# A transformer block on one core: the linear quotient written as a mean less a small term

## The chip, the cores and the metric

One core of one Trainium2 chip runs one program. The metric is device time in microseconds, the median of repeated executions; less is better. Each kernel also has one execution taken with the hardware profiler.

## The reference, cut to what matters

The input `x` is 8 batches of 512 tokens by 128 features. Four residual parts follow one another: a linear attention with 16 heads of 64 (1024 columns), an FP4 feed-forward of width 352, a causal softmax attention with 16 heads of 8, and 8 experts of which each token takes two. The part that changes is the first:

```python
q = einsum(x, wq) + bq;  k = einsum(x, wk) + bk;  v = einsum(x, wv) + bv
Q = elu(q) + 1.0;        K = elu(k) + 1.0
KV   = sum over tokens of K * v        # one number per head column
Ksum = sum over tokens of K            # one number per head column
Z    = 1.0 / (Q * Ksum + 1e-6)
attn = Q * KV * Z
out  = gelu(attn @ wo + bo)            # added to x
```

`KV` and `Ksum` are elementwise along a head's columns, so each of the 1024 columns has its own two scalars per batch.

## The kernel before, in words

The block goes through the 8 batches. Everything of the first part stands transposed: columns on the 128 partitions, the 512 tokens along the free dimension. The 1024 columns make 8 tiles of 128 by 512.

The code doesn't issue instructions where they are written. Each call makes a `Step` in a `Plan`: it records its engine, what it needs, which buffers it takes, and an estimated cost from `cost()`. The stages of a batch belong to lanes (`loads`, `norm`, `linear`, `out`, `fp4`, `attention`, `routing`, `experts`). A stage is run inside a `Span`, which gives its steps ranks that rise evenly from a low to a high number; the pairs are in the table `TURNS`, one for each lane and batch. `Plan.ordered()` then simulates the engines with the estimated costs: of the steps that could start, an engine takes the one with the lowest rank (with a bonus for the step that empties a PSUM buffer), if its buffers are free. A step on `nc.either` may go to VectorE or GpSimd. The result is one fixed order per engine, which the chip then carries out with semaphores. `SBUF` (line 661 on) lists how many buffers each tag has.

`kept_warm()` goes through that order and, where the plan shows TensorE idle, inserts at most one zero product (a matmul of `zeros` by `ident` into the PSUM tile `mid`, which adds nothing). Its length is the gap or what is missing to a share `TARGET` of a recent window, whichever is less.

In `linear_attention` (line 978), `elu` makes one tile of a feature: a matmul, a ScalarE Relu and Exp with the bias, and a VectorE combination, which gives elu without the added one. `features(c)` does this for K (the accumulated sum gives `ks`), multiplies K by v (giving `kv`), and does it for Q. ScalarE then adds one to Q, makes the divisor z = Q · Ksum + 1e-6, and scales the tile of `wo` by `kb`, the KV of that column with the bias of v in it. `products(c)` takes two tiles together, so that one reciprocal serves both:

```python
r = z0 * z1;  q0 = q0 * z1;  q1 = q1 * z0
r = 1 / r                       # two halves of 256
q0 = q0 * r;  q1 = q1 * r       # Q0/z0 and Q1/z1
```

`linear_out` (line 1031) multiplies the eight tiles by the eight scaled tiles of `wo` in two accumulations of four, adds the bias, applies gelu, transposes and adds to `x`. The FP4 stage, the softmax attention (`group`, in which a group is 4 heads), the routing and the experts follow, each in its own lane, so that the work of several batches is under way at once.

Of the kernel before, what the change touches and what calls it, by code (L numbers as in the profile page):

```python
# [134 lines left out]
class Plan:  # L135
# [51 lines left out]
    def span(self, lane, low, high):  # L187
        return Span(self, lane, low, high)
# [60 lines left out]
    def ordered(self):  # L249
# [15 lines left out]
        empties = set()  # L265
        for s in self.steps:
            for b in s.uses:
                if b.tag in self.psum and s.engine != "tensor" and (False or max(b.users, key=lambda u: u.number) is s):
                    empties.add(s)
# [14 lines left out]
        while done < len(self.steps):  # L284
            for e in self.HOP:
                while busy[e] <= now:
# [4 lines left out]
                    for s in sorted(  # L291
                        ready,
                        key=lambda s: (s.rank - (ahead if s.work > 0.6 * s.cost else 0.0) - (EMPTY if s in empties else 0.0), s.number),
                    ):
                        if s.port and port > now:
                            continue
                        asked = {}
                        for b in s.takes:
                            asked.setdefault(b.tag, []).append(b)
                        if not all(  # L300
                            all(b in turns[s.lane, t][-len(bs) :] for b in bs)
                            for t, bs in asked.items()
                        ):
                            continue
                        if all(
                            (t not in kept or stuck) and free.has(t, len(bs)) for t, bs in asked.items()
                        ):
                            best = s
                            break

                        kept.update(asked)
# [53 lines left out]
    def kept_warm(self, order):  # L365
# [11 lines left out]
        for s in order:  # L377
            if s.engine == "tensor" and self.warmer is not None:
# [6 lines left out]
                if want > 0.2 and not any(a - 0.5 < last < b + 0.1 for a, b in read):  # L385
                    n = min(512, 64 * int(want / 1.7e-3 / 64))
                    f = Step(-1, "tensor", None)
                    f.calls, f.cost, f.work = self.warmer(n), n * 1.7e-3, n * 1.67e-3
                    f.start, f.end = last, last + f.cost
                    past.append((f.start, f.end, 1.0))  # L390
                    out.append(f)
                last = s.end
# [116 lines left out]
class Span:  # L509


    def __init__(self, plan, lane, low, high):
        self.plan, self.lane, self.low, self.high = plan, lane, low, high
# [5 lines left out]
    def __exit__(self, *_):  # L519
        steps = self.plan.steps[self.first :]  # L520
        total, done = sum(s.cost for s in steps) or 1.0, 0.0
        for s in steps:
            s.rank = self.low + (self.high - self.low) * done / total
            done += s.cost
# [88 lines left out]
def cost(engine, method, out, ins, a, k):  # L613
# [32 lines left out]
    if engine == "gpsimd":  # L646
# [20 lines left out]
    ("xnT", [P, S], 2, F32),  # L667
    ("kf", [P, S], 2, F32),
    ("qf", [P, S], 7, F32),
    ("z", [P, S], 3, F32),  # L670
    ("r", [P, S], 1, F32),
    ("y", [P, S], 2, F32),
    ("wk_o", [P, D], 5, F32),
# [12 lines left out]
    ("oT", [P, NT, P], 2, F32),  # L686
# [18 lines left out]

TURNS = {
    "loads": (
        (-3.318, -1.909), (-0.316, -0.059), (0.897, 0.897), (1.614, 1.925),
        (2.836, 3.009), (4.433, 4.682), (4.978, 4.978),
    ),  # L710
    "norm": (
        (-2.124, -2.124), (-0.875, -0.875), (0.083, 0.200), (1.422, 1.904),
        (2.231, 2.231), (3.002, 3.606), (3.880, 4.108), (5.162, 5.409),
    ),
    "linear": (
        (-1.500, -0.940), (-0.500, 0.050), (0.419, 0.790), (2.088, 2.088),
        (2.612, 3.162), (3.422, 3.979), (4.158, 4.730), (4.805, 5.222),
    ),
    "out": (
        (-1.176, -0.826), (-0.386, -0.123), (0.618, 0.709), (1.508, 1.508),  # L720
        (2.508, 3.214), (3.335, 3.734), (4.601, 4.985), (5.739, 6.093),
    ),
    "fp4": (
        (-1.986, -1.736), (-0.900, -0.500), (0.154, 0.510), (1.010, 1.218),
        (2.103, 2.516), (3.487, 3.887), (3.993, 4.270), (5.177, 5.177),
        (5.602, 6.278),
    ),
    "attention": (
        (-0.500, 0.000), (0.000, 0.909), (0.934, 1.761), (2.198, 3.044),
        (3.241, 3.877), (3.954, 4.849), (5.114, 5.848), (6.017, 7.017),  # L730
        (7.193, 8.226),
    ),
    "routing": (
        (1.913, 2.213), (2.979, 3.308), (4.000, 4.223), (5.196, 5.230),
        (6.538, 6.538), (7.103, 7.746), (8.148, 8.148), (8.956, 9.346),
    ),
    "experts": (
        (2.400, 2.713), (3.217, 3.986), (4.222, 5.211), (5.438, 6.138),
        (6.531, 6.863), (7.391, 8.138), (8.571, 9.439), (9.499, 10.378),
# [5 lines left out]
def block_kernel(  # L745
# [141 lines left out]
    rank = const.tile([P, NT, E], F32, name="rank", tag="rank")  # L887
    for e in range(E):
        dev.gpsimd.memset(rank[:, :, e : e + 1], float(E - e))
# [3 lines left out]
    dev.gpsimd.memset(one_sb, 1.0)  # L893

# [83 lines left out]
    def linear_attention(b):  # L978

        xnT = normed.pop(b)  # L980

        def elu(c, i, w, tag, **accum):
# [10 lines left out]
        def features(c):  # L993

            ks, kv, kb = (new("s1", [P, 1]) for _ in range(3))
            kf = elu(c, 1, wqkv[1], "kf", accum_out=ks)
            nc.vector.tensor_scalar(ks, ks, float(S), None, ALU.add)
# [4 lines left out]
            nc.vector.scalar_tensor_tensor(pw, kf, 1.0, pw, ALU.add, ALU.mult, accum_out=kv)  # L1002

            nc.vector.tensor_scalar(
                kb, ks, bqkv_sb[:, 2, c : c + 1], kv, ALU.mult, ALU.add
            )
            qf = elu(c, 0, wqkv[0], "qf")
            nc.scalar.activation(qf, qf, AF.Identity, bias=one_sb)
            z = new("z", [P, S])
            nc.scalar.activation(z, qf, AF.Identity, bias=eps_sb, scale=ks)  # L1010
            wk_o = new("wk_o", [P, D])
            nc.scalar.activation(wk_o, wo_sb[c // 2][:, c % 2, :], AF.Copy, scale=kb)
            return qf, z, wk_o

        def products(c):


            (q0, z0, w0), (q1, z1, w1) = features(c), features(c + 1)
            r = new("r", [P, S])
            nc.either.tensor_tensor(r, z0, z1, ALU.mult)  # L1020
            nc.either.tensor_tensor(q0, q0, z1, ALU.mult)
            nc.either.tensor_tensor(q1, q1, z0, ALU.mult)
            for part in (slice(0, 256), slice(256, S)):
                nc.vector.reciprocal(r[:, part], r[:, part])
            nc.either.tensor_tensor(q0, q0, r, ALU.mult)
            nc.either.tensor_tensor(q1, q1, r, ALU.mult)
            return [(w0, q0), (w1, q1)]

        return [p for c in range(0, NC0, 2) for p in products(c)]

    def linear_out(b, pairs):
        y = new("y", [P, S])
        for half in range(2):
            po = new("ahead", [P, S])
            with together():
                for i, (wk_o, qz) in enumerate(pairs[4 * half : 4 * half + 4]):
                    nc.tensor.matmul(po, wk_o, qz, start=(i == 0), stop=(i == 3))
            if half == 0:
                nc.scalar.activation(y, po, AF.Identity, bias=bo_sb)
            else:  # L1040
                nc.vector.tensor_tensor(y, po, y, ALU.add)
# [454 lines left out]
    for b in range(NB):  # L1496
# [3 lines left out]
        pairs = stage("linear", linear_attention, b)  # L1500
        stage("out", linear_out, b, pairs)
# [80 lines left out]
```

## Time and profile before

| | |
|---|---|
| median of 3 runs | 1132.38 us (1130.52 to 1133.14) |
| the profiled execution | 1131.95 us, span 1130.1 us |
| busy: TensorE matmul, VectorE, ScalarE, GpSimd | 92%, 73%, 56%, 55% |
| mean granted TensorE clock | 0.982 |
| reciprocals on `r` | 64, 110.3 us of VectorE |
| zero products | 88 records, 40.4 us of TensorE |
| DMA | 44.31 MB, mean 39 GB/s |
| first and last reciprocal on `r` | 26.5 and 775.3 us |
| first maximum of scores in the softmax attention | 173.6 us |

Every planned instruction stands at line 407, where the plan issues it, so the profile's groups are told apart by the names of their tiles: `r`, `qf` and `z` are the linear attention, `pair` and `pr` the scores, `act` and `um` the experts. `ahead` is a PSUM bank that many stages use. An fp32 matmul of the program appears as two records. In a row of groups the numbers after the bar are busy microseconds, mean nanoseconds of one instruction, and the engine's idle time just before them with its releaser. A row of a stretch has the stretch, its length, each engine's busy time with the number of instructions, the granted TensorE clock in parts of one, the share of the DMA engines, and GB/s. A row of waits has who waited, for whom, total microseconds, how many times, and the longest.

### The profile page before, as it was taken

To read this page: it belongs to the slowest core of one execution; us is meant where nothing else is said; L and a number is where in the kernel's file an instruction comes from. 1 tells how busy PE (TensorE), PEld (TensorE's weight loads), DVE (VectorE), ACT (ScalarE), POOL (GpSimd) and SP (SyncE) were. 2 spreads that over 40 slices of the span, in tenths; PEclk is the share of its full clock that TensorE was granted. 3 is DMA by queue.
4 is the path that set the end of the run, shared out by engine and by line. 5 is a ranking of instruction groups with operands and counts; after the bars stand their busy time and mean duration, and the time that the engine had idled before them with its cause. 6 is when DMAs were issued, how large, how long until landed. Compare 5 with 4: busy or idle time off the path is not lost.

```text
span 1130.1 us, 15043 instructions
## 1 busy us (share of the span) xinstructions
PE 1040.2 (92%) x5025; PEld 488.0 (43%) x5025; DVE 830.3 (73%) x1868; ACT 630.8 (56%) x1084; POOL 624.3 (55%) x669
## 2 busy tenths in 40 slices
PE   6667788998899999999998999999999999999998
PEld 2223333344344444444543444454454445445454
DVE  6868879897888967758788968788667765556543
ACT  5756787678786644644578555764443443344311
POOL 6647846676676466237635755467644533441534
PEclk9879989999999999999999999999999999999999
DMA  8000030001101020111012000210002102001000
GB/s 235 1 1 0 1 111 1 21 20 56 39 20 30 10 94 20 58 72 35 26 39 94 19 21 20 95 30 19 20 7 98 39 20 104 21 20 30 1 10 9
DMA packets 30572, 44.31 MB, mean 39 GB/s; under 512 B 4192, under 2 KB 18464, under 8 KB 30496
## 3 DMA queue, kind: packets, MB, share of 16 engines
q1 hardware_dynamic: 30496, 43.37, 11.9%
q8 instruction: 39, 0.64, 0.2%
q14 instruction: 37, 0.30, 0.1%
HBM read 23.95 MB, written 18.87 MB: 38 GB/s over the span
## 4 chain that ended last, share of the span: by engine, by line
PE 57%; DVE 15%; ACT 6%; issue 2%; POOL 1%; DMA 0%; POOLq 0%; DVEq 0%; ACTq 0%
PE ahead L407 31%; PE pair L407 19%; PE mid L407 7%; ACT pr L407 2%; DVE r L407 2%; DVE mx L407 2%; DVE h L407 1%; DVE sc L407 1%; ACT qf L407 1%; DVE s4 routing L407 1%; DVE qf L407 1%; DVE act L407 1%; ACT z L407 1%; DVE kf L407 1%; DVE oh L407 1%
## 5 line engine op out<-in xcount | busy, mean ns | idle before, releaser
L407 ACT ACTIVATE pr<-pair 128x1024 f32<-128x1024 f32 (+1 forms) x192 | 166.7, 879 | 149.2 <-PE pair L407 129.1
L407 DVE TENSOR_REDUCE mx<-pair 128x4 f32<-128x512 f32 (+2 forms) x192 | 198.5, 1041 | 68.4 <-PE pair L407 57.7
L407 POOL TENSOR_SCALAR_AFFINE_SELECT pr<-pr 128x256 f32<-128x256 f32 (+1 forms) x192 | 92.8, 485 | 176.4 <-ACT pr L407 175.6
L407 PE MATMUL pair<-qkT 32*128 32x128 f32 (+7 forms) x1024 | 172.3, 387 | 9.4 <-ACT pr L407 2.7
L407 PEld LDWEIGHTS pair<-qkT 32*128 32x128 f32 (+1 forms) x1024 | 84.4, 183 | 181.8 <-ACT pr L407 52.0
L407 POOL TENSOR_TENSOR act<-act,tw 128x512 f32<-128x512 f32 x64 | 81.3, 1272 | 88.8 <-DVE act L407 80.6
L407 PE MATMUL ahead<-um,b_sb 128*128 128x512 f32 x240 | 122.2, 607 | 0.0
L407 DVE RECIPROCAL r<-r 128x256 f32<-128x256 f32 x64 | 110.3, 1736 | 14.9 <-POOL r L407 14.8
L407 DVE SCALAR_TENSOR_TENSOR act<-act,ahead 128x512 f32<-128x512 f32 x120 | 81.9, 684 | 51.4 <-ACT act L407 38.0
L407 POOL TENSOR_TENSOR qa<-qa,qa 128x704 f32<-128x704 f32 (+4 forms) x60 | 81.2, 1354 | 35.1 <-DVE qa L407 26.2
L407 POOL TENSOR_TENSOR qf<-qf,r 128x512 f32<-128x512 f32 x64 | 80.5, 1278 | 34.5 <-DVE r L407 27.8
L407 PE MATMUL mid<-pr,va 128*10 128x512 f32 (+3 forms) x1024 | 93.3, 435 | 0.0
L407 POOL TENSOR_TENSOR qf<-qf,z 128x512 f32<-128x512 f32 x64 | 80.3, 1270 | 0.0
L407 ACT ACTIVATE act<-ahead 128x512 f32<-128x512 f32 x60 | 35.8, 597 | 72.0 <-PE ahead L407 71.9
L407 PE MATMUL ahead<-act,a_sb 128*128 128x512 f32 x128 | 65.2, 619 | 0.0
L407 POOL TENSOR_TENSOR r<-z,z 128x512 f32<-128x512 f32 x32 | 40.9, 1278 | 41.6 <-ACT z L407 39.3
L407 PE MATMUL ahead<-tT,w_sb 128*128 128x512 f32 x120 | 63.3, 609 | 0.0
L407 ACT ACTIVATE ahead<-ahead,bqkv_sb 128x512 f32<-128x512 f32 x96 | 63.0, 656 | 0.0
L407 PE MATMUL pair<-mask_q,ident 128*128 128x128 bf16 (+1 forms) x384 | 61.6, 242 | 0.0
L407 PE MATMUL ahead<-xnT,wk 128*128 128x512 f32 x100 | 56.7, 650 | 4.8 <-DVE kf L407 2.1
L407 PEld LDWEIGHTS ahead<-um,b_sb 128*128 128x128 f32 x240 | 40.7, 190 | 36.1 <-issue 29.6
L407 ACT ACTIVATE z<-qf,eps_sb,s 128x512 f32<-128x512 f32 x64 | 51.9, 811 | 6.8 <-DVE s L407 5.1
(227 smaller groups left out, 1986.4 us busy)
## 6 DMA issues: line engine op xcount, KB each, us to landing
stacks<-qk SPq DMA_DIRECT2D x32, 512.0 KB
qkT<-stacks SPq DMA_DIRECT2D x128, 128.0 KB
x<-in SPq DMA_DIRECT2D x8, 256.0 KB
qkT<-mr SPq DMA_DIRECT2D x128, 4.0 KB
out<-x SPq DMA_DIRECT2D x8, 256.0 KB
w_sb<-in SPq DMA_DIRECT2D x3, 256.0 KB
wq<-in SPq DMA_DIRECT2D x4, 128.0 KB
wk<-in SPq DMA_DIRECT2D x4, 128.0 KB
```

The source lines that it names most:

```text
L407: getattr(e, method)(*a, **k)
```

## The change

The quotient Q · KV / (Q · Ksum + 1e-6) is written as KV/Ksum · (1 − 1e-6 / (Q · Ksum + 1e-6)). The first factor, `mean`, is one number per column, so its product with `wo` is one column of 128 numbers per batch, made by eight matmuls of one column; 1e-6 times the second part comes from the eight large matmuls, which now take 1/z in place of Q/z. Q itself is no longer multiplied. Four tiles share one reciprocal: u = z0 z1, v = z2 z3, r = 1/(u v), then u r = 1/v and v r = 1/u, and each 1/z is its partner times one of them.

`ks`, `kv` and `mean` become columns of one [128, 8] tile per batch, and the small steps are done for two columns at once; part of them move to GpSimd. The bias of v is added to `mean`. In `linear_out` the two sums are scaled by −1e-6, and the mean column with the output bias is added by one more ScalarE pass.

Beside it: `Span` takes three ranks (low, middle, high), and `TURNS` has new numbers throughout; buffer counts change; `kept_warm` fills pauses longer than 1.5 us in the plan to four fifths, with several zero products of up to 512 columns; the bonus of a step that empties a PSUM buffer is worked out from the buffers that steps take; some constants are set in another order at the start.

```diff
 def kept_warm(self, order):
...
                 want = min(gap, TARGET * Clock.WINDOW - worked)
-                if want > 0.2 and not any(a - 0.5 < last < b + 0.1 for a, b in read):
+
+                if gap > 1.5:
+                    want = max(want, 0.8 * gap)
+                while want > 0.2 and not any(a - 0.5 < last < b + 0.1 for a, b in read):
                     n = min(512, 64 * int(want / 1.7e-3 / 64))
...
                     out.append(f)
+                    last, want = f.end, want - f.cost
...
 class Span:
...
-            s.rank = self.low + (self.high - self.low) * done / total
+            x = done / total
+            s.rank = (
+                self.low + (self.middle - self.low) * 2 * x if x < 0.5
+                else self.middle + (self.high - self.middle) * (2 * x - 1)
+            )
...
-    ("xnT", [P, S], 2, F32),
+    ("xnT", [P, S], 1, F32),
     ("kf", [P, S], 2, F32),
-    ("qf", [P, S], 7, F32),
-    ("z", [P, S], 3, F32),
-    ("r", [P, S], 1, F32),
+    ("qf", [P, S], 9, F32),
+    ("heads", [P, NC0], 9, F32),
+    ("r", [P, S], 3, F32),
     ("y", [P, S], 2, F32),
-    ("wk_o", [P, D], 5, F32),
+    ("wk_o", [P, D], 8, F32),
...
-    ("oT", [P, NT, P], 2, F32),
+    ("oT", [P, NT, P], 1, F32),
...
     "linear": (
-        (-1.500, -0.940), (-0.500, 0.050), (0.419, 0.790), (2.088, 2.088),
-        (2.612, 3.162), (3.422, 3.979), (4.158, 4.730), (4.805, 5.222),
+        (-2.201, -1.936, -0.881), (-0.300, -0.221, 0.045), (0.497, 0.804, 0.804),
+        (0.986, 1.377, 1.660), (1.833, 2.674, 2.781), (3.805, 3.805, 3.936),
+        (4.303, 4.555, 4.830), (5.338, 5.653, 5.869),
     ),
...
 def linear_attention(b):
...
+        ks, kv, mean = (new("heads", [P, NC0]) for _ in range(3))
...
         def features(c):
-
-            ks, kv, kb = (new("s1", [P, 1]) for _ in range(3))
-            kf = elu(c, 1, wqkv[1], "kf", accum_out=ks)
-            nc.vector.tensor_scalar(ks, ks, float(S), None, ALU.add)
+            kf = elu(c, 1, wqkv[1], "kf", accum_out=ks[:, c : c + 1])
...
-            nc.vector.scalar_tensor_tensor(pw, kf, 1.0, pw, ALU.add, ALU.mult, accum_out=kv)
-
-            nc.vector.tensor_scalar(
-                kb, ks, bqkv_sb[:, 2, c : c + 1], kv, ALU.mult, ALU.add
+            nc.vector.scalar_tensor_tensor(
+                pw, kf, 1.0, pw, ALU.add, ALU.mult, accum_out=kv[:, c : c + 1]
             )
-            qf = elu(c, 0, wqkv[0], "qf")
-            nc.scalar.activation(qf, qf, AF.Identity, bias=one_sb)
-            z = new("z", [P, S])
-            nc.scalar.activation(z, qf, AF.Identity, bias=eps_sb, scale=ks)
-            wk_o = new("wk_o", [P, D])
-            nc.scalar.activation(wk_o, wo_sb[c // 2][:, c % 2, :], AF.Copy, scale=kb)
-            return qf, z, wk_o
+            return elu(c, 0, wqkv[0], "qf")
+
+        def divisors(c):
+            z = [features(c + i) for i in range(2)]
+            two = slice(c, c + 2)
+            nc.vector.tensor_scalar(ks[:, two], ks[:, two], float(S), None, ALU.add)
+            for i in range(2):
+                nc.scalar.activation(z[i], z[i], AF.Identity, bias=one_sb)
+                nc.scalar.activation(
+                    z[i], z[i], AF.Identity, bias=eps_sb, scale=ks[:, c + i : c + i + 1]
+                )
+            nc.vector.tensor_scalar(mean[:, two], ks[:, two], 1e-15, None, ALU.max)
+            nc.vector.reciprocal(mean[:, two], mean[:, two])
+            nc.gpsimd.tensor_tensor(mean[:, two], kv[:, two], mean[:, two], ALU.mult)
+            nc.gpsimd.tensor_tensor(
+                mean[:, two], mean[:, two], bqkv_sb[:, 2, two], ALU.add
+            )
+            return z
 
         def products(c):
-            (q0, z0, w0), (q1, z1, w1) = features(c), features(c + 1)
-            r = new("r", [P, S])
-            nc.either.tensor_tensor(r, z0, z1, ALU.mult)
-            nc.either.tensor_tensor(q0, q0, z1, ALU.mult)
-            nc.either.tensor_tensor(q1, q1, z0, ALU.mult)
-            for part in (slice(0, 256), slice(256, S)):
-                nc.vector.reciprocal(r[:, part], r[:, part])
-            nc.either.tensor_tensor(q0, q0, r, ALU.mult)
-            nc.either.tensor_tensor(q1, q1, r, ALU.mult)
-            return [(w0, q0), (w1, q1)]
-
-        return [p for c in range(0, NC0, 2) for p in products(c)]
+            u, v, r = (new("r", [P, S]) for _ in range(3))
+            z = divisors(c)
+            nc.either.tensor_tensor(u, *z, ALU.mult)
+            z += divisors(c + 2)
+            nc.either.tensor_tensor(v, *z[2:], ALU.mult)
+            nc.either.tensor_tensor(r, u, v, ALU.mult)
+            for some in (slice(0, 256), slice(256, S)):
+                nc.vector.reciprocal(r[:, some], r[:, some])
+            nc.either.tensor_tensor(u, u, r, ALU.mult)
+            nc.either.tensor_tensor(v, v, r, ALU.mult)
+            out = []
+            for i, other in enumerate((v, v, u, u)):
+                nc.either.tensor_tensor(z[i], z[i], other, ALU.mult)
+                wk_o = new("wk_o", [P, D])
+                nc.scalar.activation(
+                    wk_o, wo_sb[(c + i) // 2][:, i % 2, :], AF.Copy,
+                    scale=mean[:, c + i : c + i + 1],
+                )
+                out.append((wk_o, z[i ^ 1]))
+            return out
+
+        return mean, [p for c in range(0, NC0, 4) for p in products(c)]
 
-    def linear_out(b, pairs):
+    def linear_out(b, mean, pairs):
...
             if half == 0:
-                nc.scalar.activation(y, po, AF.Identity, bias=bo_sb)
+                nc.scalar.activation(y, po, AF.Copy, scale=-1e-6)
             else:
-                nc.vector.tensor_tensor(y, po, y, ALU.add)
+                nc.vector.scalar_tensor_tensor(y, po, -1e-6, y, ALU.mult, ALU.add)
+
+        pc = new("ahead", [P, 1])
+        with one_go():
+            for c in range(NC0):
+                nc.tensor.matmul(
+                    pc, wo_sb[c // 2][:, c % 2, :], mean[:, c : c + 1],
+                    start=(c == 0), stop=(c == NC0 - 1),
+                )
+        same = new("s1", [P, 1])
+        nc.vector.tensor_tensor(same, pc, bo_sb, ALU.add)
+        nc.scalar.activation(y, y, AF.Identity, bias=same)
```

The other seven lanes of `TURNS` change in the same way, from two to three numbers per turn.

## The prediction, on record before the result

> **What bounds the kernel now.** I read the page's busy shares first, then the slices, then the same engines in four stretches, then what TensorE waited for in the first of them.
>
> ```profile
> PE 1040.2 (92%) x5025; PEld 488.0 (43%) x5025; DVE 830.3 (73%) x1868; ACT 630.8 (56%) x1084; POOL 624.3 (55%) x669
> PE   6667788998899999999998999999999999999998
> DVE  6868879897888967758788968788667765556543
> PEclk9879989999999999999999999999999999999999
> PE 57%; DVE 15%; ACT 6%; issue 2%; POOL 1%; DMA 0%; POOLq 0%; DVEq 0%; ACTq 0%
> ```
>
> TensorE is the bound, but not everywhere: its row begins at 6 and reaches 9 only after a fifth of the span, and the granted clock is lower there. The stretches say it in microseconds:
>
> ```profile
> core 0: us, PE busy (x) PEld busy (x) DVE busy (x) ACT busy (x) POOL busy (x), PEclk, DMA share, GB/s
> 0.00:170.00 170.00, 124.68 (x306) 53.66 (x307) 127.36 (x346) 115.77 (x207) 105.60 (x129) 0.91 0.20 58
> 170.00:400.00 230.00, 211.38 (x1053) 97.12 (x1052) 202.55 (x439) 167.26 (x294) 153.30 (x151) 0.99 0.08 26
> 400.00:850.00 450.00, 436.90 (x2302) 208.03 (x2301) 338.99 (x754) 251.11 (x428) 250.43 (x267) 1.00 0.13 43
> 850.00:1130.00 280.00, 267.30 (x1368) 129.17 (x1366) 161.43 (x332) 96.62 (x156) 114.93 (x125) 0.99 0.10 32
> ```
>
> TensorE idles 45.3 us in the first stretch (the head, before the first score maximum at 173.6 us), 18.6 in the second, 13.1 and 12.7 in the rest. Of what it calls busy, 16.7, 9.7, 2.0 and 12.1 us are zero products. Elsewhere a microsecond more on TensorE is a microsecond more of time; in the head it is mostly hidden. What TensorE waited for in the head:
>
> ```profile
> PE ahead L407 <- ACT xn L407: 11.8, 2, 9.3
> PE ahead L407 <- DVE kf L407: 8.6, 6, 2.5
> PE pair L407 <- DVE kf L407: 5.2, 3, 3.0
> PE pair L407 <- DVE s L407: 2.9, 3, 2.2
> PE pair L407 <- DVE h L407: 2.2, 2, 1.8
> ```
>
> About half ends at VectorE (8.6 + 5.2 + 2.9 + 2.2 and smaller ones, 22 of 45); 11.8 us is a hole of order, batch 1's norm coming late. The rows that the change touches:
>
> ```profile
> L407 DVE RECIPROCAL r<-r 128x256 f32<-128x256 f32 x64 | 110.3, 1736 | 14.9 <-POOL r L407 14.8
> L407 POOL TENSOR_TENSOR qf<-qf,z 128x512 f32<-128x512 f32 x64 | 80.3, 1270 | 0.0
> L407 POOL TENSOR_TENSOR qf<-qf,r 128x512 f32<-128x512 f32 x64 | 80.5, 1278 | 34.5 <-DVE r L407 27.8
> L407 POOL TENSOR_TENSOR r<-z,z 128x512 f32<-128x512 f32 x32 | 40.9, 1278 | 41.6 <-ACT z L407 39.3
> L407 DVE TENSOR_SCALAR s<-s,bqkv_sb,s 128x1 f32<-128x1 f32 x64 | 17.3, 270 | 2.0
> ```
>
> **The change, part by part.**
>
> *VectorE, linear stage.* 64 half-tile reciprocals become 32: −32 × 1.736 = −55.6 us. Per tile the `ks + S` (0.145) and `kb` (0.270) go; per two tiles come an add and a max on two columns (nearest row 0.145 each) and a two-column reciprocal (0.177 on four columns). 64 × 0.415 − 32 × 0.467 = −11.6. Eight bias adds of one column, +1.2. Sum −66 us of 830. What that is worth depends on the stretch. Head: 19 halves and 21 tiles lie there, so 9.5 × 1.736 + 21 × 0.18 = 20 us are freed; half of TensorE's waits end at VectorE, so I take −10 (ends: −20, and 0 if another engine is then late). Second stretch: 25 halves and 24 tiles, 26 us freed, but TensorE has only 18.6 us of idle to give back; half of it, −9.3 (−18.6 to 0). Third: 20 halves freed against 13.1 us of idle, in waits none of which is above 1.1 us there; −3 (−6 to 0). Last: no linear work, 0.
>
> *TensorE.* The 24 feature products and 8 output products a batch stay. New is the mean: eight products of 128x128 by one column. Nearest is the routing gate's, 128x8: its eight instructions begin at 359.95 and the next group at 360.86, 0.112 us each with the weight load, two to a product. So 64 × 2 × 0.112 = 14.3 us on the bounding engine. About 21 of 64 tiles fall in the head, where TensorE idles; two thirds remain on the path: +9.6 (0 to +14.3).
>
> *GpSimd.* Full products go from 20 to 18 a batch: −16 × 1.27 = −20 us, since all of them ran on GpSimd. 64 two-column products come; the rows bound one by 0.10 (a memset of four columns) and 1.02 (a power of four columns); the 256- and 512-column products (0.726, 1.276) put the intercept at 0.18, nearest in operation: +11.5. Near even, hidden at 55% busy. The last of these now stands before ScalarE's `wk_o` copies, and on ScalarE's queue everything planned later stands behind those; `wk_o` is wanted only with the end products, so 0, and if that cover is gone 0.4 us a copy.
>
> *The chain of one group.* This is the price. Today, after the last z: one product, two halves, two products, 1.27 + 3.47 + 2.54 = 7.3 us. Then, after the fourth z: v, r, two halves, u·r, v·r and four end products, 2.54 + 3.47 + 2.54 + 5.08 = 13.6 us on GpSimd. +6.35, and the out stage gets one more 512-column ScalarE pass (0.687 with a bias): +7.0 per batch. In full stretches other lanes cover it. In the head, batch 0's linear → out → fp4 → attention is what everything waits for: +7.0 (0 if VectorE takes half the products; +21 if all three of the head's batches pay). Three `r` buffers hold one group, so the next group's first product waits for the last end product; its z's sit in nine `qf`.
>
> The Trainium skill speaks against this chain. On products on GpSimd the row `qf<-qf,r` has 1.260 at the least, 1.270 in the middle, one of 1.719. "SBUF — State Buffer" (two separate sides) says that GpSimd and a VectorE operation with two SBUF inputs take their shared port as an exclusive lock for a whole instruction; by that rule, one 0.69 us VectorE operation before each of the six would be an estimated 4 us more, and the term 11 in place of 7. A mean of 1.278 shows no such queueing, so the row decides.
>
> *Zero products.* Planned pauses over 1.5 us are now filled to four fifths, with several products each. 34 records lie in the head at present. The head's clock is 0.91: 124.7 × 0.09 = 11.2 us of TensorE time. ScalarE idles 54 us there, 18 of it for TensorE, so a third counts: −4. (−11; or a loss: a product of 512 columns holds the queue 0.86 us if the next one is ready.)
>
> By "TensorE: Matmul & The Clock Gate" (why this matters) idle gaps above about 3 us drop the clock to half. The head has four such gaps (9.3, 3.8, 3.2, 3.0); one half-rate window of 3.4 us after each would be an estimated 7 us. The row says more, 11, and the clock was 0.66 in 140 to 150 us with TensorE 92% busy, so gaps alone don't explain it.
>
> *Table and buffers.* The new table moves every lane, loads included (their queue takes 11.9% of the DMA engines: hidden). The trace can't show its effect. A hole like the 11.8 us may close or open; I take a quarter, −3 (−12 to +12). One `xnT` and one `oT` in place of two: ScalarE's copy into them now waits for the last reader. In the head the last reader of batch 0's `xnT` starts at 50.1 and the next copy at 63.0; for `oT` four transposes of 0.27 against some 28 us between groups: 0 (up to +3).
>
> **Sum.** +9.6 − 10 − 9.3 − 3 + 7.0 − 4 − 3 = −12.7 us on the profiled execution's 1131.95 (span 1130.1 and 1.85 around it), 0.4 below the median 1132.38: **1119 us**.
>
> **Rivals.**
> A. VectorE really is what holds the first 400 us (75 and 88% busy). Then all 20 and all 18.6 come off: 9.6 − 20 − 18.6 − 3 + 7 − 4 − 3 = −32, 1100 us. For it: the second stretch. Against: the waits there are short and of many kinds.
> B. TensorE's small waits after 170 us stay, whoever is late. Second and third gains fall away: −0.4, 1131.5 us.
> C. Slower: the four-tile chain sets the head. GpSimd's run of 13.6 us ends last in each of its three batches, so 3 × 7.0 = 21, and the head's relief is nothing, since VectorE wasn't last, nor does the table help: 9.6 − 9.3 − 3 + 21 − 4 = +14, 1146 us. It decides once more than 2.8 batches' chains (19.7 / 7.0) lie open. For it: GpSimd is 62% busy in the head and already waits 10.4 us there for z. Against: plain products may go to VectorE at 0.69.
> D. The zero products land where TensorE would work. Another 29 (as many as the first two stretches have), each half in the way, cost 29 × 0.43 = 12.5, and the clock's 4 are not won: 1136 us.
>
> **How the numbers follow.** Forecast 0.50 (own range 1108 to 1128), A 0.16, B 0.07, C 0.21, D 0.06. Faster by over 0.2% (some 2.3 us, about what a measurement of this kernel can tell from none): 0.66; within it 0.07; slower 0.27. The range takes in half of A and of C: 1099 to 1146.
>
> **What would show it.** Reciprocals on `r` x32 and VectorE near 764 us; 128 records of one column, 0.112 us apart; GpSimd near 615; head idle of TensorE clearly under 45 us with a clock above 0.95; over 400 us no more idle than now. If products on `r` and `qf` are followed by long TensorE waits for GpSimd before 200 us, C is right; many more zero products with the following product's operands long ready, D. The prediction fails above all if the table's order costs or saves more than the 12 us allowed it.

## The result: 1143.8 us, slower by 1%

The changed kernel takes 1143.78 us in the median (1139.39 to 1147.38, four executions), the kernel before 1132.14 beside it: a ratio of 1.0101, with a 95% interval of 1.0080 to 1.0123. The forecast was 1119, in a range of 1099 to 1146. Its profiled execution is the slowest of the four, 1147.38 us with a span of 1145.7; it is the one read here.

The page after: busy shares, three rows of slices and the chain that ended last.

```profile
PE 1079.8 (94%) x5217; PEld 515.8 (45%) x5217; DVE 798.7 (70%) x1812; ACT 634.6 (55%) x1092; POOL 615.7 (54%) x717
PE   7888789999799999999998999989999999999998
DVE  6777677878977796657777766668767774675442
PEclk9999998999999899999999999999999999999989
PE 71%; DVE 16%; ACT 9%; issue 2%; POOL 1%; DVEq 0%; ACTq 0%; POOLq 0%
```

TensorE's row now begins at 7 and 8 in place of 6, and the clock of the head reads 9 nearly throughout. VectorE lost 31.6 us, not the 66 of the forecast. TensorE's busy time rose by 39.6 us. The same four stretches:

```profile
core 0: us, PE busy (x) PEld busy (x) DVE busy (x) ACT busy (x) POOL busy (x), PEclk, DMA share, GB/s
0.00:170.00 170.00, 140.67 (x397) 64.51 (x397) 117.85 (x333) 121.12 (x218) 103.81 (x144) 0.98 0.18 54
170.00:400.00 230.00, 214.73 (x1026) 97.90 (x1027) 183.98 (x386) 164.68 (x289) 143.66 (x167) 0.94 0.08 27
400.00:850.00 450.00, 437.51 (x2336) 210.22 (x2335) 326.73 (x731) 247.81 (x424) 237.45 (x269) 1.00 0.13 42
850.00:1145.00 295.00, 286.84 (x1461) 143.17 (x1459) 170.13 (x364) 100.96 (x164) 130.74 (x138) 0.99 0.10 34
```

In the head, idle TensorE fell from 45.3 to 29.3 us and the clock rose from 0.91 to 0.98. In the second stretch idle fell from 18.6 to 15.3, but the clock dropped from 0.99 to 0.94, and TensorE has fewer product records (1026 against 1053) in the same 230 us. Zero products went from 40.4 to 66.5 us. The first 170 us of them, before and after (the busy times are TensorE's, its weight loads' and GpSimd's):

```profile
0.00:170.00 170.00, 16.65 (x34) 7.15 (x34) 0.13 (x1) 0.91 0.20 58
0.00:170.00 170.00, 35.80 (x84) 16.80 (x84) 0.13 (x1) 0.98 0.18 54
```

They rose by 19.1 us where idle time fell by 16.0, so the fall of idle time in the head is no sign by itself that TensorE waits less for work.

The rows of the linear part after the change, with all shapes apart (busy us, mean ns | idle before):

```profile
L414 DVE RECIPROCAL r<-r 128x256 f32<-128x256 f32 x32 | 55.0, 1735 | 5.9 <-POOL r L414 5.9
L414 POOL TENSOR_TENSOR r<-r,r 128x512 f32<-128x512 f32 x48 | 60.7, 1276 | 22.3 <-DVE r L414 14.2
L414 PE MATMUL ahead<-heads,wo 128*128 128x1 f32 x128 | 14.9, 246 | 0.0
L414 DVE TENSOR_SCALAR heads<-heads 128x2 f32<-128x2 f32 x64 | 32.9, 514 | 1.2
L414 DVE RECIPROCAL heads<-heads 128x2 f32<-128x2 f32 x32 | 5.3, 165 | 1.0
```

The reciprocals, GpSimd's products and the mean products are as counted. The fourth row isn't: the adds and maxima of two columns take 0.514 us each, where 0.145 was taken. The view of the tile gives their least, middle and greatest duration in ns:

```profile
L414 DVE TENSOR_SCALAR heads<-heads x64: 104/172/1711, 19.9 to 833.8; 128x2 f32<-128x2 f32 x64
```

Half of them take 0.17 us or less, some over 1.2. The longest, in the timelines of VectorE and GpSimd side by side (start, length):

```profile
241.31 1.71 DVE L414 TENSOR_SCALAR heads<-heads 128x2 f32<-128x2 f32 x1
241.31 1.69 POOL L414 TENSOR_TENSOR qa<-qa,qa 128x704 f32<-128x704 f32 x1
```

It starts with a product of GpSimd that has nothing to do with it, and ends 0.02 us after it. Of the 64, the 36 that overlap a GpSimd product take 0.770 us in the mean, the other 28 take 0.185 (worked out from the two engines' starts and ends in the trace). The twelve longest, 1.19 us and more, each end 0.02 to 0.03 us after a GpSimd product.

**Where the time lies.** To compare kernels whose orders differ, I counted TensorE's useful work: every matmul record at its full-clock issue time by its number of columns, zero and mean products with nothing. It sums to 880 us in each kernel. The table gives the time in the span at which so much of it had begun; the two last columns are runs of the section below. Each column is one profiled execution, with mean clocks of 0.982, 0.982, 0.993 and 0.982, and the count knows small products only roughly: differences of a microsecond mean nothing.

| useful work, us | before | changed | changed, single columns | before + pairs |
|---|---|---|---|---|
| 50 | 105.5 | 94.3 | 93.4 | 107.8 |
| 100 | 183.8 | 179.2 | 177.2 | 186.6 |
| 150 | 249.6 | 252.2 | 243.4 | 255.1 |
| 200 | 317.1 | 319.3 | 306.4 | 323.1 |
| 300 | 437.0 | 452.6 | 436.8 | 443.3 |
| 500 | 674.4 | 685.6 | 669.9 | 682.5 |
| 800 | 1032.0 | 1041.9 | 1025.5 | 1040.1 |

The changed kernel was 11 us ahead in the first part of the head, had given that back by 250 us of its span, and was 16 us behind at 450 us. After that it gains a little again.

### The profile page after: what moved, and what is told of

Its sections match the earlier page's. It is cut to its first block, busy times and chain, and to the rows that moved or that the text cites. A ratio compares the mean times of both kernels' runs of the same rounds, so it can differ in the third digit from the quotient of the medians.

```text
span 1145.7 us, 15381 instructions
## 1 busy us (share of the span) xinstructions
PE 1079.8 (94%) x5217; PEld 515.8 (45%) x5217; DVE 798.7 (70%) x1812; ACT 634.6 (55%) x1092; POOL 615.7 (54%) x717
## 4 chain that ended last, share of the span: by engine, by line
PE 71%; DVE 16%; ACT 9%; issue 2%; POOL 1%; DVEq 0%; ACTq 0%; POOLq 0%
PE ahead L414 37%; PE pair L414 25%; PE mid L414 10%; ACT qf L414 2%; DVE mx L414 2%; DVE heads L414 2%; DVE kf L414 1%; DVE h L414 1%; DVE qf L414 1%; DVE sc L414 1%; DVE r L414 1%; ACT ahead L414 1%; ACT pair L414 1%; ACT kf L414 1%; DVE ahead L414 1%
## 5 line engine op out<-in xcount | busy, mean ns | idle before, releaser
L414 PE MATMUL pair<-qkT 32*128 32x128 f32 (+7 forms) x1024 | 176.9, 391 | 6.9 <-DVE mx L414 4.3
L414 DVE SCALAR_TENSOR_TENSOR act<-act,ahead 128x512 f32<-128x512 f32 x116 | 79.3, 684 | 46.2 <-ACT act L414 30.0
L414 PE MATMUL mid<-pr,va 128*10 128x512 f32 (+3 forms) x1024 | 96.0, 446 | 0.4 <-POOL pr L414 0.4
L414 POOL TENSOR_TENSOR r<-r,r 128x512 f32<-128x512 f32 x48 | 60.7, 1276 | 22.3 <-DVE r L414 14.2
L414 PE MATMUL mid<-zeros,ident 128*128 128x512 f32 (+7 forms) x152 | 66.5, 564 | 3.8 <-POOL zeros L924 3.8
L414 PE MATMUL ahead<-act,a_sb 128*128 128x512 f32 x120 | 59.2, 612 | 0.0
L414 DVE RECIPROCAL r<-r 128x256 f32<-128x256 f32 x32 | 55.0, 1735 | 5.9 <-POOL r L414 5.9
L414 PE MATMUL ahead<-xnT,wv 128*128 128x512 f32 x100 | 54.4, 626 | 2.8 <-DVE qf L414 1.4
L414 ACT ACTIVATE qf<-qf,eps_sb,heads 128x512 f32<-128x512 f32 x64 | 50.8, 810 | 7.6 <-DVE heads L414 6.9
L414 POOL TENSOR_TENSOR r<-qf,qf 128x512 f32<-128x512 f32 x32 | 40.7, 1273 | 26.6 <-ACT qf L414 26.3
```

The lines of the kernel that those rows point to most:

```text
L414: getattr(e, method)(*a, **k)
```

## The experiments

Three suspects stood at the start: L, the two-column steps, which wait for GpSimd; Z, the zero products, in the way of work; C, the granted clock, lower where TensorE is the bound. A fourth, T, is the table of turns. Kernels that keep the order of every engine are compared directly; where the order changes too, the text says so.

### The changed kernel again

No edit.

> The changed kernel itself once more, so that its edits below are compared on one chip. All theories: 1.008 to 1.012 of the kernel before, near 1143.8 us, with a spread of several us between executions (1139 to 1147 so far).

1142.18 us (1133.28 to 1149.97), ratio 1.0089 (1.0055 to 1.0122). The executions of this one program spread by 17 us, and their time follows the granted clock: 1133.28 at 0.997, 1139.69 at 0.991, 1145.83 at 0.983, 1149.97 at 0.981. A straight line through these eight and the four of the first comparison (correlation 0.98) has 9.4 us for each hundredth of clock and 1131.1 us at full clock. The kernel before spreads by 5 us here, at 0.980 to 0.986. But its time follows the clock too: its 71 executions beside the runs of this section (1126.2 to 1134.3 us at 0.980 to 0.989) have 6.7 us for each hundredth (correlation 0.78), and their line ends at 1119.9. Below, "at full clock" means such a line's end; it is an extrapolation wherever no execution came near 1, and for the kernel before a long one.

### The zero products by the old rule

```diff
-                if gap > 1.5:
-                    want = max(want, 0.8 * gap)
-                while want > 0.2 and not any(...):
+                if want > 0.2 and not any(...):
...
-                    last, want = f.end, want - f.cost
```

> The changed kernel with the old rule for zero products: at most one in a pause, not over the gap or what the window lacks. The order of all other instructions is the changed kernel's. Theory Z, that the added zero products hold TensorE while its next product is ready (66.5 us of them instead of 40.4, and in the first 12 us a row of them behind which batch 0's transposes wait 3.5 us): 8 to 12 us come back, about 1134 us. Theory M, that TensorE pays for the mean's 128 one-column products and the zeros only fill idle time: no gain, or a loss of some 4 us by a lower clock in the head, 1143 to 1148 us.

1144.65 us, ratio 1.0107 (1.0090 to 1.0124): no gain. The order is untouched, since zero products go in after the planning. The first 170 us of it:

```profile
0.00:170.00 170.00, 133.49 (x345) 59.47 (x345) 114.14 (x326) 115.69 (x209) 98.16 (x140) 0.92 0.16 45
```

The head's clock fell to 0.92 and 16 us of its zero products went. By the count of useful work the run is some 5 us behind the changed kernel at 100, and level with it at 850. As run, Z falls as a cause of the loss, and so does the forecast's gain of 4 us by this rule. At equal clock it is open: these six executions had 0.973 to 0.979, and their line ends at 1125.0, 6 below the changed kernel's, far from anything measured.

### Two columns issued as single columns

```diff
+    def one_by_one(self):
+        (method, a, k), = self.steps[-1].calls
+        self.steps[-1].calls = [
+            (method, [x[:, i : i + 1] if isinstance(x, View) else x for x in a], k)
+            for i in range(2)
+        ]
...
             nc.vector.tensor_scalar(ks[:, two], ks[:, two], float(S), None, ALU.add)
+            plan.one_by_one()
...
             nc.vector.tensor_scalar(mean[:, two], ks[:, two], 1e-15, None, ALU.max)
+            plan.one_by_one()
```

> The changed kernel with the two VectorE steps on two columns (the add of 512 and the max) issued as two steps of one column each, in the same places. Theory L, that a two-column step waits for GpSimd's running product (514 ns in the mean and 1711 at most, where the one-column step of the kernel before took 145): the 64 steps fall from 32.9 us to 128 of about 0.145, 18.6 us, none above 0.4, and 3 to 6 us of time come back, 1138 to 1141 us. Theories Z and M: the steps may get shorter, the time stays within 2 us of the changed kernel's.

1130.00 us (1127.85 to 1137.32), ratio 0.9990 (0.9975 to 1.0006). The loss is gone, with twice as many instructions: 12.2 us come back against the 1142.18 beside it, more than twice what L expected. Its row of groups:

```profile
L421 DVE TENSOR_SCALAR heads<-heads 128x1 f32<-128x1 f32 x128 | 13.5, 147 | 0.0
```

Its first two stretches, in the columns of the result's table:

```profile
0.00:170.00 170.00, 142.50 (x401) 65.55 (x402) 114.77 (x363) 122.94 (x221) 105.50 (x147) 0.98 0.19 56
170.00:400.00 230.00, 218.62 (x1081) 102.63 (x1080) 184.92 (x436) 172.64 (x305) 155.51 (x175) 0.99 0.11 36
```

The steps take 0.147 us in the mean and 0.155 at most, whatever GpSimd does. The second stretch holds 1081 records in place of 1026, at a clock of 0.99. At full clock the line ends at 1121.9 us, 9.2 below the changed kernel's 1131.1; at 0.991, which both had, 1130.89 stands against 1139.6. L holds. The other 3 us as run went with the clock, and this profile has no long half-clock stretch; the executions of the twelve with the lowest clock, 0.984 and 0.987, took 1137.32 and 1133.55.

### One mean product in place of eight

Seven of the eight products of `mean` by `wo` are left out in each batch, so seven eighths of the mean are missing from the output.

```diff
+        method, a, k = plan.steps[-1].calls[0]
+        plan.steps[-1].calls = [(method, a, {"start": True, "stop": True})]
         same = new("s1", [P, 1])
```

> The changed kernel with one of the eight one-column products of the mean per batch; the other seven are left out, so seven eighths of the mean's sum are missing from the output. All else stands in the same order. Theory M: 112 records at 0.112 us go from the bounding engine, 12.5 us, of which 9 to 12 come back, about 1133 us. Theory Z: less than 4 us come back, since TensorE would wait anyway.

1131.29 us, ratio 1.0017 (0.9998 to 1.0035). As run 10.9 us come back against 1142.18, within M's 9 to 12, but not by M's cause. At full clock the line ends at 1128.5: the seven products cost 2.6 us, not most of 12.5. The other 8 us of the gain went with the clock. This profile has no half-clock window between 170 and 400 us, where the changed kernel's first has 27 us of them; the second stretch of this run:

```profile
170.00:400.00 230.00, 212.37 (x1043) 97.20 (x1042) 195.41 (x413) 171.76 (x304) 154.53 (x174) 1.00 0.11 35
```

### All pauses filled, with pairs and with single columns

```diff
-SLACK, TARGET = 0.0, 0.6
+SLACK, TARGET = 0.0, 1.0
```

> The changed kernel with zero products in nearly every pause that the plan sees over 0.2 us (TARGET 1.0 in place of 0.6), all else in the same order; 82 groups of them in place of 53. Theory G, that the changed kernel's loss is the TensorE clock, which stands at half for 27 us between 170 and 400 us of its profile where little is multiplied, while the kernel before has its 31 us at half in the head, where TensorE idles anyway: the clock of 170 to 400 us rises from 0.94 to 0.97 or more and 5 to 10 us come back, 1132 to 1138 us, with less spread between executions. Theory Z, that zero products hold TensorE: some 29 more of them cost up to 0.4 us each, 1145 to 1155 us.

1140.92 us, ratio 1.0098 (1.0077 to 1.0119). The clock came back, 0.997 in the profile; the time didn't, and G's 1132 to 1138 is missed. By 1126 us the zero products take 87.8 us in place of 61.7, and the line ends at 1136.7, 5.6 above the changed kernel's. So filling buys clock at about the price that the clock is worth.

> The same together with the two-column VectorE steps issued one column at a time. If lock and clock are separate causes, as the executions of the changed kernel and of the single columns suggest (1131 us and 1122 us when their times are carried to a full clock), both come off: 1120 to 1127 us, faster than both kernels. If the single columns had won only by keeping TensorE's clock, nothing is added: 1129 to 1132 us.

With single columns as well: 1133.45 us, ratio 1.0029 (1.0005 to 1.0052), above both ranges. The line ends at 1127.7 against 1121.9 without the filling: the same price.

### The new sum with the old table, and the old sum with the new

In the first, the old ranks stand in the new three-rank form, with the mean of low and high in the middle. In the second, the old sum, its buffers and its zero rule get the new `TURNS` and `Span`. Both change the order on every engine.

> The changed kernel with the old table of ranks (the middle rank halfway, so that ranks rise evenly as before); sum, buffers and zero rule are the new ones, the order is planned anew. Theory T, that the new table put thin softmax work where nothing dense stands beside it: fewer than 10 us at half clock after 170 us and 1125 to 1136 us. Theory S, that the new sum itself brings the loss (two-column waits, mean products, a longer chain): 1140 us or more.

1171.79 us, ratio 1.0369 (1.0344 to 1.0393). The profile has 48 us of half clock after 170 us, where T asked for less than 10.

> The kernel before with the new table and its three-rank spans; sum, buffers and zero rule are the old ones. Theory T: over 15 us at half clock between 170 and 400 us and 1140 us or more. Theory S: within 0.5% of the kernel before, 1127 to 1138 us.

1145.65 us, ratio 1.0136 (1.0109 to 1.0163). The time is in T's range, but the profile has no half clock between 170 and 400 us, where T asked for over 15.

T as a cause of the loss falls: the new table is worth 28 us to the new sum (1171.8 − 1143.8), and costs the old one 14.6 (against 1131.06 beside it). Each fits its own sum. The forecast's −3, with 12 either way, was too sure: what an order is worth isn't a term that can be added to the others.

### Extra steps of two columns, and of one, in the kernel before

This measures the disputed cost by itself, in the kernel before. Behind each add on the key sums one more is issued, on a constant:

```diff
             nc.vector.tensor_scalar(ks, ks, float(S), None, ALU.add)
+            plan.steps[-1].calls.append(
+                ("tensor_scalar", (spare[:, 0:2], ident[:, 0:2], 1.0, None, ALU.add), {})
+            )
```

> The kernel before, its order untouched; behind each of the 64 adds of one column on the key sums VectorE issues one more add, of two columns of a constant into a spare tile that nobody reads. Theory L (an fp32 VectorE step of two columns waits for GpSimd's running product; one of one column doesn't): the new steps take some 0.5 us in the mean and over 1.5 us at the most, VectorE gains 25 us or more, and the time rises by 5 to 12 us, to 1137 to 1144. Rival (the long two-column steps belong to the changed kernel's order, where they happen to stand behind its own GpSimd chain): they take about 0.15 us here, VectorE gains 10, and the time stays within 3 us, 1129 to 1135.

> The control of the run beside it: the same kernel before with the same 64 extra adds, of one column in place of two. Theory L: 0.145 us each with none above 0.3, VectorE gains 9.3 us, the time rises by 0 to 4, to 1131 to 1136. Rival (any extra small step on VectorE costs as much, whatever its width): the time is that of the run with two columns within 2 us.

With two columns 1140.42 us, ratio 1.0082 (1.0064 to 1.0099), or 9.1 us for 64 steps that nobody reads. With one column 1131.67, ratio 1.0004 (0.9991 to 1.0017). The tile view of the run with pairs (least/middle/greatest ns):

```profile
L407 DVE TENSOR_SCALAR spare<-ident x64: 153/240/1274, 17.4 to 763.3; 128x2 f32<-128x2 f32 x64
```

The same view of the run with single columns:

```profile
L407 DVE TENSOR_SCALAR spare<-ident x64: 138/144/146, 17.6 to 753.1; 128x1 f32<-128x1 f32 x64
```

The 42 pairs that overlap a GpSimd product take 0.579 us, the other 22 take 0.158. The 39 and 25 single columns on either side of that division take 0.143 and 0.144. The pairs' mean, 0.435, is 27.8 us in sum. VectorE's busy time rose by 19.0, less than the 25 expected, and the greatest duration, 1.274, is below the 1.5 expected; the time is inside its range. 64 steps whose result is never used cost 9 us of kernel time once they have two columns, and one column in the same place costs nothing clear of noise: L is shown, in an order that has nothing of the change. In the table of useful work this kernel falls behind over the whole linear part, by 2 us at 50, 6 at 200, 8 at 500.

### Single columns with one mean product

Both edits together; again seven eighths of the mean are left out.

> The changed kernel with its two-column adds and maxima issued as single columns, and also only one of the eight mean products of a batch (the mean of seven of eight tiles is left out of the sum). If the two costs are separate, they add up: at full granted clock 1121.9 - 2.6 = 1119.3, and as run 1119 to 1124. Rival (both take away the same TensorE pauses between 170 and 400 us, so that the second brings nothing): 1127 to 1131, as with single columns alone.

1128.98 us (1120.81 to 1129.68), ratio 0.9964 (0.9945 to 0.9983), above the range as run. The line ends at 1119.3, the sum of the two savings, and the execution with the highest clock, 0.998, took 1120.81. But eleven of the twelve ran below that, most at 0.989, and the profile has one half-clock stretch of 17 us at 366, in its row of the stretch 365 to 383:

```profile
365.00:383.00 18.00, 17.95 (x70) 7.68 (x71) 9.54 (x24) 9.62 (x15) 8.47 (x12) 0.53 0.00 0
```

The costs add up at equal clock, as expected; the rival's time came out as run, with a lower clock and not by the rival's cause.

### Single columns with the old rule for the first pause

```diff
+                first = last == 0.0
-                if gap > 1.5:
+                if gap > 1.5 and not first:
...
-                    last, want = f.end, want - f.cost
+                    last, want = f.end, 0.0 if first else want - f.cost
```

> The changed kernel with single columns; only the first pause of the plan, before batch 0's transposes, is filled as in the kernel before (one zero product in place of a row of them); every other pause as changed. If the row of zero products at the start is what makes batch 0 late, its transposes begin near 8.4 us in place of 11.9, and the time falls by 2 to 3 us against single columns alone: 1126 to 1128. Rival (batch 0 has slack, or the clock of the first 30 us falls and takes it back): 1129 to 1132.

1129.14 us (1126.40 to 1129.83), ratio 0.9981 (0.9970 to 0.9992), the only complete kernel here whose interval lies below 1, by 0.2%; the 1126 to 1128 expected are missed. TensorE's timeline with single columns alone (start, length):

```profile
3.86 8.87 PE L421 MATMUL mid<-zeros,ident 128*128 128x512 f32 x16 [3.86 <-POOL zeros L931]
12.56 0.60 PE L421 MATMUL ahead<-ident,xn 128*128 128x128 f32 x4
```

And with the first pause by the old rule as well:

```profile
3.86 2.08 PE L422 MATMUL mid<-zeros,ident 128*128 128x512 f32 x2 [3.86 <-POOL zeros L932]
8.40 1.63 PE L422 MATMUL ahead<-ident,xn 128*128 128x128 f32 x4 [2.47 <-ACT xn L422]
```

Batch 0's transposes start 4.2 us sooner. In useful work this kernel is 2.1 us ahead of single columns alone at 50 and 2.4 at 800, so in these two profiles the row of zero products at the start delays everything. At 850 that lead is gone; between the two lies a half-clock stretch of 6.8 us at 1070. Whether it falls there because of this edit is open. Against single columns the runs don't separate the two (0.9981 and 0.9990, intervals overlapping).

## Why the prediction was wrong

The forecast was −12.7 us and the measurement +11.7, 24.4 apart. One term accounts for 9.2 us of that at full clock and for 12.2 as run, as much as the whole slowdown. The rest is a gain that didn't come, and the runs don't divide it among the other terms.

**The step that failed first: "an add and a max on two columns (nearest row 0.145 each)".** The row was of one column. 64 steps took 32.9 us in place of 9.3. Issued one column at a time, they gave 12.2 us of kernel time back as run, 9.2 at full clock. That the adds stand in the chain from the key sum to the divisor isn't needed for this cost: the extra pairs in the kernel before, which nobody reads, cost 9.1. The trace of before had a nearer row, which the forecast didn't read, here from its groups:

```profile
L407 DVE TENSOR_SCALAR s4 fp<-mv fp 128x4 f32<-128x4 f32 x8 | 3.0, 372 | 0.3
```

and from its tile view:

```profile
L407 DVE TENSOR_SCALAR s4 fp<-mv fp x8: 170/170/1261, 75.6 to 843.4; 128x4 f32<-128x4 f32 x8
```

Four columns: a middle of 0.170 and one of 1.261. The two long ones of these eight, 1.261 and 0.694, end 0.02 to 0.03 us after a GpSimd product. A middle and a greatest value that far apart are here the sign of a wait inside the instruction, and a mean hides it.

The forecast did weigh the rule of the Trainium skill, "SBUF — State Buffer" (two separate sides), but only for the big products and only for VectorE operations with two SBUF inputs; the same sentence of the page also names a VectorE operation in a two-port mode. (Its estimate there counted six GpSimd products; the chain that it prices has eight. It isn't in the sum.) It dismissed the rule because GpSimd's products showed no queueing. That is still so: theirs took 1.276 us in the mean. The rule says that the one that starts first holds the shared port and the other waits; here the waits fell on VectorE. Looking at one side of a lock doesn't exclude it. The same page (who interferes with whom) names `tensor_scalar` among the operations that can take the second port, and "VectorE: DVE Perf Modes" (Mode 2×_2P; what auto-detection checks) gives the condition: one source, source and destination in SBUF, and an outermost dimension other than one that is even in both, or equal in both. One column has no dimension to split and two have; the runs agree, with 0.144 against 0.435 us. The planner misses it too: line 217 marks a one-source step as a user of the port only from 17 elements on, so it was free to plan these steps beside GpSimd's products.

**The second step that failed: the clock term, "−4".** The forecast treated it as a matter of the head. The head's clock did rise, from 0.91 to 0.98. But half-clock time between 170 and 400 us went from 3.4 to 27.3 us. It moved: both profiled executions have 41.0 us of it in their spans and a mean clock of 0.982, so no gain was left. Within the changed kernel the time follows the clock, and its line ends 12.7 us below its median. That is not 12.7 of the difference to the kernel before, whose own line ends 11.7 below 1131.58, the median of its 71 executions. At the same mean clock, 0.988, the kernel before took 1126.2 to 1126.6 us and the changed one 1143.8. So the mean clock doesn't explain why the changed kernel is slower. What could is that half clock costs more between 170 and 400 us than in the head, where 30.7 of the 41.0 us lay before; but that price wasn't measured, and the head isn't free of it: TensorE spent 21.5 of those 30.7 us on products other than zeros. The changed kernel's stretches around five of the windows:

```profile
190.00:198.00 8.00, 8.00 (x18) 3.18 (x18) 4.77 (x9) 2.33 (x4) 1.72 (x4) 0.57 0.01 2
207.00:212.00 5.00, 5.00 (x24) 2.48 (x23) 4.20 (x7) 1.56 (x4) 3.08 (x5) 0.66 0.00 0
245.00:249.00 4.00, 4.00 (x16) 1.23 (x17) 3.28 (x7) 0.78 (x2) 2.21 (x4) 0.60 0.42 131
310.00:314.00 4.00, 4.00 (x8) 1.42 (x7) 3.93 (x10) 2.42 (x4) 0.87 (x3) 0.58 0.00 0
382.00:396.00 14.00, 13.97 (x64) 5.28 (x64) 9.64 (x22) 7.84 (x12) 8.04 (x11) 0.63 0.00 1
```

TensorE counts as busy in all of them. Before the second lie the 16 one-column records of a mean; before the last, score products of 32 and 34 rows. That the small products bring the clock down isn't shown: in the profile without seven eighths of the mean products the windows went, with single columns they mostly went too, and with both one of 17 us stood at 366. The trigger is open.

Point by point, the rest:

- *VectorE relief in the head, "−10".* The direction was right, the size is open. TensorE's idle time that ended at VectorE fell there from 22 to 14 us, and only to 19 by the old rule for zero products; the 16 us less of idle time, which the forecast named as a sign, are covered by 19.1 more of zero products. Useful work was 11 us ahead at 50, and as much by the old rule with its clock of 0.92; with pairs the lead was 4.6 at 100, with single columns 6.6. How much of it is the new order's isn't separated.
- *Second and third stretch, "−9.3" and "−3".* Not won by the changed kernel: idle time fell by 3.3 and 0.6 us, and rival B described it better. With single columns it fell by 7.2 and 1.5 (18.6 to 11.4, 13.1 to 11.6), near the forecast, but useful work stands level with before at 300 (436.8 against 437.0) and 6.5 ahead at 800. So whether that became kernel time is open.
- *Mean products, "+9.6".* The count and the 0.112 us were right, the place was not: seven eighths cost 2.6 us at equal clock, about 3 for all. In the full stretches most of it lay in short waits that remain without it: TensorE's idle time there is 17.6 and 15.5 us without the seven, 15.3 and 12.5 with them.
- *The chain of four tiles, "+7.0".* Its sign as a bound of the head didn't come: the longest waits of TensorE before 170 us are the first zero product's (for the constant it reads, set once by GpSimd), and waits for VectorE and ScalarE; none is for a product on `r` or `qf` by GpSimd. The longest in the first 170 us:

```profile
PE mid L414 <- POOL zeros L924: 3.8, 1, 3.8
PE pair L414 <- DVE h L414: 3.4, 3, 2.2
PE ahead L414 <- DVE kf L414: 3.3, 6, 0.9
PE pair L414 <- ACT pair L414: 3.2, 3, 1.7
```

  Rival C named 1146 us, near the measured time, by a cause of which these waits show no sign; that nearness is luck. Whether the chain costs its 7 us wasn't tested by itself.
- *Zero products in the way (rival D).* As run the old rule brought nothing back; about 2.4 us of it hold at the very start. At equal clock it is open, as said there.
- *The table, "−3".* Not separable from the sum it was made for, as the exchange showed.
- *VectorE near 764, GpSimd near 615.* 798.7 and 615.7. Of the 34.7 us of VectorE, 23.6 are the pairs; the remainder is no single row and wasn't followed.

With single columns, the changed order stands at 1130.00 as run, 2.0 below the kernel before beside it and not 12.7. At full clock its line ends at 1121.9, the kernel before's at 1119.9: no gain there either, as far as that long extrapolation goes. So beyond the pairs, the forecast's gains and costs came to about nothing together, and why isn't shown.

## What to carry to other kernels

Price a small instruction by a row of its own shape, and look at the least, middle and greatest duration: if they are far apart, the mean is that of a wait, and the wait may belong to the other engine of a shared port. Before merging two one-column steps on VectorE into one of two columns beside a busy GpSimd, count what a full GpSimd product costs when it comes first; two instructions were cheaper than one by 9 us over 64. And where a kernel's time follows the granted clock, compare two kernels at the same clock, and carry both to full clock or neither: one kernel's line here suggests a second cause of 12.7 us, and the other kernel's line takes it away.

## What the runs showed of the hardware

- An fp32 add of 128x2 on VectorE, SBUF to SBUF, took 0.158 us where no GpSimd product ran beside it and 0.579 in the mean where one did (extra steps in the kernel before). The longest add or max of the changed kernel took 1.711 and ended 0.02 us after the product. The add on 128x1 took 0.143 to 0.144 in both cases. A reciprocal of 128x2 took 0.165, and 0.167 at most beside a product.
- The granted clock has two levels in these records, full and half, and half clock comes in stretches that are multiples of 3.4 us. One hundredth of the mean clock went with 9.4 us of 1140 in the changed kernel and with 6.7 in the kernel before.
- Half clock was granted with TensorE busy for 17.95 of 18.00 us (single columns with one mean product). The Trainium skill, "TensorE: Matmul & The Clock Gate" (why this matters), puts the drop down to idle gaps above about 3 us; the trace of that run has no wait of TensorE above 0.5 us between 345 and 386, so gaps alone don't explain it here.
- Eight executions of one program spread over 17 us, in step with a granted clock of 0.981 to 0.997.
